# Reciprocals of softmax totals as powers on GpSimd instead of reciprocals on VectorE

## The chip, the core and the metric

The kernel runs on one NeuronCore of a Trainium2 chip. Its engines run their own instruction queues side by side and wait for each other through semaphores: TensorE (PE in the profile; its weight loads are PEld), VectorE (DVE), ScalarE (ACT), GpSimd (POOL), and SyncE (SP), which issues nearly all DMAs here. The metric is the device time of one execution in microseconds. Before the change it is 3157.24 us, the median of three runs (3157.11, 3157.24 and 3159.02).

## What is computed

Two attention blocks stand one after the other, on x of shape (8, 512, 32, 32) in float32: 8 batch items, 512 channels, 1024 positions. The change touches the softmax of the first block, which has 8 heads of 64 channels.

```python
# layer 0
hn = group_norm(x, gn1_scale, gn1_bias)              # 32 groups
qkv = einsum('bchw,oc->bohw', hn, w_qkv) + b_qkv
q, k, v = split(qkv.reshape(b * 8, 3 * 64, 1024), 3, axis=1)
wgt = softmax(einsum('bct,bcs->bts', q * 64 ** -0.25, k * 64 ** -0.25), axis=-1)
a = einsum('bts,bcs->bct', wgt, v)
x = x + group_norm(einsum('bchw,oc->bohw', a, w_proj) + b_proj, gn2_scale, gn2_bias)
# layer 1: weights normalised by row, qkv divided by its root mean square over
# channels, one head of 512 channels, softmax over 1024 positions
x = (x + w_out @ attention(x)) * 2 ** -0.5
```

## The kernel before

The kernel goes through the 8 batch items one after the other. For each it runs 32 steps of the first block's attention, then the first block's output projection and norm, then the second block; the steps of the next item begin while the last products of the second block are still being made. Every instruction is pinned to the order in which the program issues it on its engine (class InOrder, so most instructions carry its line, L34), and the order across engines comes from semaphores alone.

**A step.** Step i is one block of 128 query positions of one pair of heads: 4 pairs times 8 blocks make the 32 steps (STEPS, NB = 8). The two heads of a pair lie in the upper and lower 64 partitions of the queries and keys (tile qk) and are the two halves, hh = 0 and 1, of everything that follows. The method `step` (lines 635 to 650) issues, in this order:

- `softmax(i)`: for each head, VectorE takes the maximum of the scores in PSUM over 1024 keys, negated (TENSOR_REDUCE, nm<-s); ScalarE writes the exponentials to the tile p (128 partitions, both heads, 1024 keys each) and sums them into one column of the tile tot (called tt in the profile) by its accumulator. The accumulator comes out with a short instruction of its own behind the exponential, ACTIVATION_READ_ACCUMULATOR.
- `values(g)`, every second step: the products of values and transposed weights (po<-pT,v) for the two steps that were five and four steps back (LAG = 5).
- fills: a share of the projections that make the queries and keys of the next pair of heads, or leftovers of the second block.
- `scores(i + 1)`: TensorE's eight matmuls for the next step's scores, into two of three PSUM tiles (ps_s, three buffers).
- `turn()`: VectorE transposes the weights of the step before, in blocks of 32x32, from p into the tile pb (STREAM_TRANSPOSE, 128x2048), and SyncE copies them by four DMAs into pT.
- `scale()`: the weights of this step are multiplied by the reciprocals of their totals. VectorE makes the reciprocals of both heads, and GpSimd makes one scaling for each head (TENSOR_SCALAR, p<-p,tt).
- later work: additions on GpSimd that finish the queries and keys of the next pair (qk<-qk, qk<-qk,v, qk<-qk,spare), the normalisation of the next item's input (hn<-hn,a,c), and in the last eight steps of an item sums for the next item's values (tv<-hn, tv<-hn,tv).

So on VectorE the order in a step is: two maxima, the transposition of the step before, the reciprocal. On GpSimd it is: two scalings, then the later work, in one queue. The transposition of step i is issued in step i + 1, behind that step's maxima, and it waits for both scalings of step i.

**Buffers.** p and pb have two buffers each, the totals and negated maxima three each. The exponentials of step i + 2 go into the p of step i, which the transposition must have read.

**Pairs of heads.** Queries and keys of the next pair are put together on GpSimd in the last steps of the pair before, from pieces that ScalarE copies out of PSUM (`project_seven`, from the second batch item on; the first item and each item's first pair use `project_rows`, with fewer additions). TensorE's scores of the next pair's first step read them.

Of the kernel before, what the change touches and what calls it, by code (L numbers as in the profile page):

```python
# [8 lines left out]
F32 = mybir.dt.float32  # L9
I32 = mybir.dt.int32  # L10
AF = mybir.ActivationFunctionType
ALU = mybir.AluOpType
AX = mybir.AxisListType
P = 128
# [38 lines left out]
def attention_blocks_kernel(  # L53
# [38 lines left out]
    const = ctx.enter_context(tc.tile_pool(name="const", bufs=1))  # L92
# [12 lines left out]
    PE, VE, AC, PO, SY = (InOrder(tc, e) for e in (nc.tensor, nc.vector, nc.scalar, nc.gpsimd, nc.sync))  # L105
# [81 lines left out]
    for g in range(P // SQ):  # L187
        VE.tensor_copy(same[:, g * SQ : (g + 1) * SQ], flat)
    VE.tensor_scalar_mul(same2, same, 2.0 ** 0.5)
    shift = const.tile([P, 1], F32, name="shift")  # L190
    VE.memset(shift, -16.0)
    cols = const.tile([P, NCOLS], F32, name="cols")
# [79 lines left out]
    def turn(wrows, dst, k, scale=1.0):  # L272

        for half in range(2):
            pt = ps_s.tile([P, 2, CI, P], F32, tag="sc", name=f"wT_{k}_{half}")
            for jj in range(2):
                for ci in range(CI):
                    PE.transpose(pt[:, jj, ci, :], wrows[:, 2 * half + jj, ci * P : (ci + 1) * P], ident)
            o = dst[:, :, 2 * half * P : 2 * (half + 1) * P].rearrange("p ci (jj o) -> p jj ci o", jj=2)
            for jj in range(2):  # L280
                if jj:
                    AC.activation(o[:, jj], pt[:, jj], AF.Copy, scale=scale)
                else:
                    VE.tensor_scalar_mul(o[:, jj], pt[:, jj], scale)
# [267 lines left out]
    class Heads:  # L552
# [49 lines left out]

        def scale(self):
            i, p, tot = self.now
            VE.reciprocal(tot, tot)
            for hh in range(2):
                PO.tensor_scalar(p[:, :, hh, :], p[:, :, hh, :], tot[:, hh : hh + 1], 1.0, ALU.mult, ALU.mult)
            self.waiting = (i, p)

# [310 lines left out]
    class Layer1:  # L920
# [10 lines left out]
        def project(self, hn_next):  # L931
# [45 lines left out]
            def score_unit(m):  # L977

                w = near["score"]
                c = {f"{i + 1}{th + 1}": u[:, m + 2 * i, halves_[th]] for i in range(2) for th in range(2)}  # L980

                def last(which):
                    def scale(to=c[which], by=rrow[:, halves_[int(which[1]) - 1]]):
                        PO.tensor_mul(to, to, by)

                    if self.rrow is None:
                        waiting.append(scale)
                    else:
                        scale()

                return Seven(
                    f"u_{b}_{m}", HN,
                    lambda k, h: w[:, k, h, m * P : (m + 1) * P], self.right(slice(0, HN)), c, last,
                )
# [622 lines left out]
```

## Time and profile before

The profile is of one execution, which took 3158.3 us; its span from the first to the last instruction is 3156.5 us.

| engine | busy us | share of the span | instructions |
|---|---|---|---|
| TensorE, matmuls (PE) | 3128.6 | 99% | 13014 |
| TensorE, weight loads (PEld) | 1613.1 | 51% | 13014 |
| VectorE (DVE) | 2366.4 | 75% | 3213 |
| GpSimd (POOL) | 1409.5 | 45% | 1129 |
| ScalarE (ACT) | 1070.1 | 34% | 1844 |

The groups of instructions that the steps are made of, over all 256 steps:

| instruction | engine | count | busy us | mean ns |
|---|---|---|---|---|
| maximum, nm<-s, 128x1024 | VectorE | 512 | 602.2 | 1217 |
| transposition, pb<-p, 128x2048 | VectorE | 256 | 590.0 | 2305 |
| reciprocal, tt<-tt, 128x2 | VectorE | 256 | 32.2 | 126 |
| exponential, p<-s,nm, 128x1024 | ScalarE | 512 | 565.6 | 1109 |
| scaling, p<-p,tt, 128x1024 | GpSimd | 512 | 566.0 | 1118 |

How to read what follows: a line of the timeline begins with the start in microseconds from the span's start and the length; several like instructions in a row are merged, with their number behind an x. In brackets stands the idle time of the engine before the instruction and what ended it. A line of a stretch has its bounds, its length, the busy time of the engine with the number of instructions, the granted TensorE clock as a share of full speed, the busy share of the DMA engines and what they moved in GB/s. The granted clock is 0.998 over the span.

The second batch item's first maximum starts at 488.58 us and that of its last step at 657.45 us.

### The profile page before, as it was taken

How to read it: one execution, taken by the hardware profiler on the slowest of the kernel's cores; microseconds unless marked ns; L12 is line 12 of the kernel's file. 1: busy time of each engine (PE TensorE's matmuls, PEld its weight loads, DVE VectorE, ACT ScalarE, POOL GpSimd, SP SyncE). 2: the span in 40 equal slices, each digit the busy share in tenths (PEclk: the TensorE clock that was granted, in tenths of full speed). 3: DMA queues.
4: the chain of work that ended last, by engine and by line, in shares of the span. 5: the costliest groups of instructions: out<-in, count | busy, mean ns of one | idle time of the engine just before them, and what ended most of it. 6: DMA issues, size and time to landing. Idle time of an engine off the chain costs nothing.

```text
span 3156.5 us, 36568 instructions
## 1 busy us (share of the span) xinstructions
PE 3128.6 (99%) x13014; PEld 1613.1 (51%) x13014; DVE 2366.4 (75%) x3213; ACT 1070.1 (34%) x1844; POOL 1409.5 (45%) x1129
## 2 busy tenths in 40 slices
PE   9999999999999999999999999999999999999899
PEld 5445544456444554545545555445554455444454
DVE  5697777876788767886678876787677877778765
ACT  2453124521245212551125502354133531245311
POOL 1554236732367314771247703566235642356124
PEclk9999999999999999999999999999999999999999
DMA  6777225862168521784128832388224872158600
GB/s 207 208 203 232 77 57 158 215 203 67 57 180 230 178 55 60 206 231 153 47 79 227 225 117 51 114 219 227 91 68 119 217 230 77 30 159 213 194 7 33
DMA packets 230317, 451.56 MB, mean 143 GB/s; under 512 B 22100, under 2 KB 62840, under 8 KB 224376
## 3 DMA queue, kind: packets, MB, share of 16 engines
q1 hardware_dynamic: 230016, 449.20, 50.4%
q8 instruction: 104, 1.70, 0.2%
q14 instruction: 77, 0.63, 0.1%
q10 hardware_dynamic: 120, 0.02, 0.0%
HBM read 137.26 MB, written 29.56 MB: 53 GB/s over the span
## 4 chain that ended last, share of the span: by engine, by line
PE 88%; DMA 3%; POOL 3%; DVE 3%; SPq 1%; issue 1%; ACT 0%; DVEq 0%; ACTq 0%; POOLq 0%
PE s L34 12%; PE po L34 12%; PE p L34 7%; PE p_v_T L34 6%; PE pq L34 6%; PE p_v_B L34 5%; PE py L34 4%; PE pqk L34 4%; PE pa L34 4%; PE p_u_T L34 4%; PE pe_e L34 3%; PE pe_bc L34 3%; PE pe_a L34 3%; PE p_o_T L34 3%; PE p_u_B L34 3%; DMA pT<-pb 2%
## 5 line engine op out<-in xcount | busy, mean ns | idle before, releaser
L34 ACT ACTIVATE p<-s,nm 128x1024 f32<-128x1024 f32 x512 | 565.6, 1109 | 796.0 <-DVE nm L34 461.0
L34 POOL TENSOR_SCALAR p<-p,tt 128x1024 f32<-128x1024 f32 x512 | 566.0, 1118 | 413.5 <-DVE tt L34 405.4
L34 DVE TENSOR_REDUCE nm<-s 128x1 f32<-128x1024 f32 x512 | 602.2, 1217 | 138.1 <-PE s L34 137.0
L34 DVE STREAM_TRANSPOSE pb<-p 128x2048 f32<-128x2048 f32 x256 | 590.0, 2305 | 54.7 <-DMA pT<-pb 36.2
L34 PE MATMUL s<-qk 64*128 64x512 f32 x2048 | 510.5, 605 | 0.7 <-POOL qk L34 0.5
L34 PE MATMUL po<-pT,v 128*64 128x256 f32 x4096 | 473.4, 383 | 2.4 <-DMA pT<-pb 1.5
L34 PEld LDWEIGHTS po<-pT,v 128*64 128x64 f32 x4096 | 283.2, 137 | 228.5 <-issue 29.9
L34 PEld LDWEIGHTS s<-qk 64*128 64x128 f32 x2048 | 193.2, 186 | 242.7 <-issue 214.5
L34 PE MATMUL p<-e,v 128*128 128x512 f32 (+1 forms) x520 | 229.9, 594 | 2.5 <-DVE x L34 2.5
L34 POOL TENSOR_TENSOR x<-x,o 128x1024 f32<-128x1024 f32 x21 | 52.1, 2509 | 349.0 <-ACT o L34 349.0
L34 POOL TENSOR_TENSOR esum<-esum,e 128x512 f32<-128x512 f32 x96 | 141.6, 1499 | 148.3 <-ACT e L34 148.3
L34 POOL TENSOR_TENSOR u<-u,xy 128x512 f32<-128x512 f32 x64 | 79.2, 1268 | 278.1 <-DMA xy<-far_rinv 273.5
L34 PE MATMUL pq<-hn,qk 64*128 64x512 f32 (+1 forms) x420 | 191.8, 593 | 0.0
L34 ACT ACTIVATE e<-e,shift,rinv 128x512 f32<-128x512 f32 x96 | 75.8, 810 | 269.0 <-DVE e L34 269.0
L34 DVE TENSOR_TENSOR v<-v,p_v_T 128x256 f32<-128x256 f32 x300 | 114.3, 416 | 68.8 <-PE p_v_T L34 50.0
L34 PEld LDWEIGHTS p<-e,v 128*128 128x128 f32 x520 | 98.1, 192 | 130.5 <-issue 121.3
L34 PE MATMUL pqk<-hn,qk 64*128 64x512 f32 (+1 forms) x672 | 158.2, 590 | 0.0
L34 PE MATMUL pq<-t,qk 64*128 64x512 f32 x336 | 151.0, 589 | 0.0
L34 PE MATMUL pq<-v,qk 64*128 64x512 f32 x336 | 150.9, 589 | 0.0
L34 POOL TENSOR_TENSOR esum<-e 128x512 f32<-128x512 f32 x16 | 25.1, 1586 | 274.7 <-ACT e L34 274.7
L34 PE MATMUL py<-x,gram 128*128 128x512 f32 x320 | 141.2, 601 | 4.4 <-DVE x L34 4.4
L34 POOL TENSOR_TENSOR qk<-qk,v 128x512 f32<-128x512 f32 x96 | 127.2, 1334 | 3.2 <-ACT v L34 1.6
(240 smaller groups left out, 4737.7 us busy)
## 6 DMA issues: line engine op xcount, KB each, us to landing
pT<-pb SPq DMA_DIRECT2D x1024, 256.0 KB, 4.6
qk<-far_qk SPq DMA_DIRECT2D x21, 896.0 KB
hn<-in_x_dram SPq DMA_DIRECT2D x32, 512.0 KB, 4.8
x<-in_x_dram SPq DMA_DIRECT2D x32, 512.0 KB, 3.9
out_dram<-x SPq DMA_DIRECT2D x63, 256.0 KB, 2.8
score<-far_score SPq DMA_DIRECT2D x8, 1792.0 KB, 11.8
value<-far_value SPq DMA_DIRECT2D x8, 1792.0 KB
proj<-far_proj SPq DMA_DIRECT2D x7, 1792.0 KB
```

Source lines behind the costliest of these rows:

```text
L34: return lambda *args, **kw: self._pin(call(*args, **kw))
```

## The change

The reciprocal on VectorE is gone. In its place GpSimd raises each head's total to the power -1, one TENSOR_TENSOR on 128x1 against a constant column of -1.0, in front of that head's scaling. Each power waits for ScalarE's accumulator of its own head; each scaling waits for the power in front of it on the same engine. The constant is filled once by GpSimd at the start.

```diff
@@ constants
     VE.tensor_scalar_mul(same2, same, 2.0 ** 0.5)
+    minus = const.tile([P, 1], F32, name="minus")
+    PO.memset(minus, -1.0)
     shift = const.tile([P, 1], F32, name="shift")
     VE.memset(shift, -16.0)
@@ class Heads
         def scale(self):
             i, p, tot = self.now
-            VE.reciprocal(tot, tot)
             for hh in range(2):
+                PO.tensor_tensor(tot[:, hh : hh + 1], tot[:, hh : hh + 1], minus, ALU.pow)
                 PO.tensor_scalar(p[:, :, hh, :], p[:, :, hh, :], tot[:, hh : hh + 1], 1.0, ALU.mult, ALU.mult)
             self.waiting = (i, p)
```

The order of the other instructions on each engine stays as it was. Waits that the reciprocal's wait for ScalarE had covered move to other instructions: nearly all of VectorE's maxima now name ScalarE beside TensorE, for a negated maximum that ScalarE read three steps before.

## The prediction

> **What bounds the kernel now.** I read the page from the top: engine shares first, then the chain that ended last, then the group of instructions that the change touches.
>
> ```profile
> PE 3128.6 (99%) x13014; PEld 1613.1 (51%) x13014; DVE 2366.4 (75%) x3213; ACT 1070.1 (34%) x1844; POOL 1409.5 (45%) x1129
> ...
> PE 88%; DMA 3%; POOL 3%; DVE 3%; SPq 1%; issue 1%; ACT 0%; DVEq 0%; ACTq 0%; POOLq 0%
> ...
> L34 POOL TENSOR_SCALAR p<-p,tt 128x1024 f32<-128x1024 f32 x512 | 566.0, 1118 | 413.5 <-DVE tt L34 405.4
> ```
>
> PE is busy for 99% of the span and makes 88% of the chain. Nothing that another engine does faster can bring much: PE's idle time is 3156.5 - 3128.6 = 27.9 us in all. The third line is what the change aims at: POOL stands idle for 405 us in front of its scalings, and the reciprocals (tile tt) end that wait. The views of waits say whether anyone pays for it.
>
> ```profile
> POOL p L34 <- DVE tt L34: 405.4, 198, 9.5
> ...
> PEld s L34 <- ACT p L34: 13.6, 36, 0.9
> ...
> PEld s L34 <- POOL qk L34: 5.1, 11, 0.8
> ```
>
> Columns: us in total, times, longest. POOL's wait is long, but PE's weight loads for the scores wait for the softmax only 13.6 us in the whole kernel, and 5.1 us for the additions that POOL makes on queries and keys. So POOL's 405 us are slack, not loss, and the question turns round: how much of that slack do the added instructions use up? One steady step, from the timeline (start, length, engine):
>
> ```profile
> 649.05 2.30 DVE L34 STREAM_TRANSPOSE pb<-p 128x2048 f32<-128x2048 f32 x1
> 651.28 0.12 DVE L34 RECIPROCAL tt<-tt 128x2 f32<-128x2 f32 x1
> ...
> 654.58 2.30 DVE L34 STREAM_TRANSPOSE pb<-p 128x2048 f32<-128x2048 f32 x1
> ...
> 649.84 1.27 POOL L34 TENSOR_TENSOR tv<-hn,tv 128x512 f32<-128x512 f32 x1
> 651.50 2.21 POOL L34 TENSOR_SCALAR p<-p,tt 128x1024 f32<-128x1024 f32 x2 [0.39 <-DVE tt L34]
> ...
> 650.20 0.20 ACT L34 ACTIVATION_READ_ACCUMULATOR p<-s,nm 128x1 f32 x1
> ```
>
> The totals of both heads are out at 650.40; the reciprocal starts at 651.28 because the transposition stands ahead of it. Scaling ends at 653.71, and the transposition that reads its result starts at 654.58, 0.87 us later.
>
> **Removed.** 256 reciprocals of 0.12 us from DVE. Next on DVE are the maxima, which in steady steps wait for PE's scores anyway, so nothing is won there. In the few steps after a change of head pair, where DVE runs without pause, the reciprocal overlaps its neighbours and costs about 0.06 us (651.28 against the transposition's end at 651.35, then to 651.40); steps there last 4.7 us, 935.34 to 940.04 from maximum to maximum; some five of them in seven batch items give 35 x 0.06 = 2 us. The ceiling of any gain through the softmax is the 13.6 us above.
>
> **Moved.** The first scaling no longer waits for the transposition before it. No DMA is issued by the step itself; SP's copies follow the transposition as before, and PE's order is untouched. The scaling now runs beside the transposition: the addition at 649.84 lies wholly inside the one at 649.05 and takes 1.27 us, the common length of such additions, so I charge nothing for it. The Trainium skill (GPSIMD Engine Reference, section Key points) speaks against the move: GpSimd shares its SBUF interfaces with VectorE and contends with some of its instructions. Taken at its worst, scaling would be held until the transposition ends, nothing would start earlier, and the powers would come on top in full; the row above shows no such hold for an addition, and none shows it for a scaling.
>
> **Added.** One memset at the start (beside the weight loads, nothing), and 512 powers on 128x1, each followed by a scaling that must see its result. That hand-over costs 0.08 us: the additions x<-x,v read what the instruction before them wrote, and 30 of them have 2.4 us of idle time in front. The power itself is in no row. Lower end: an addition of no width.
>
> ```profile
> L34 POOL TENSOR_TENSOR x<-x,v 128x512 f32<-128x512 f32 x30 | 38.4, 1281 | 2.4
> ...
> L34 POOL TENSOR_TENSOR s_qk<-qk 64x2048 f32<-64x2048 f32 x1 | 4.5, 4526 | 0.0
> ```
>
> From about 1.27 us at 512 columns to 4.53 at 2048 the line rises 2.12 ns a column and meets zero at 0.18 us (its long row has half the partitions). A power is far more than an addition, so 0.18 is the floor. Upper end: 1.27 us, a whole 512-column addition; a power on one column would then cost as much as some 500 additions on a column. No row says where between them it lies; I take the middle, 0.73 us, so c = 0.81 us for a power with its hand-over (ends 0.26 and 1.35).
>
> The Trainium skill prices no power. Its table in GPSIMD Engine Reference, Elementwise — side-by-side cycle accounting, puts GpSimd at 1.96 times VectorE for an addition; twice the reciprocal's 0.12 us would be 0.24 us, c = 0.32, and the sum below would come to 3155 us.
>
> **POOL's idle time against c.** Stretches of the second batch item's 32 steps, cut at ends of scalings (length, POOL busy):
>
> ```profile
> 112.94:284.26 171.32, 101.76 (x91) 1.00 0.80 213
> 494.80:517.45 22.65, 16.60 (x14) 1.00 0.49 134
> 517.45:538.28 20.83, 16.84 (x15) 1.00 0.84 215
> 538.28:580.18 41.90, 29.30 (x26) 1.00 0.83 223
> 580.18:621.70 41.52, 29.30 (x26) 1.00 0.84 216
> 621.70:664.38 42.68, 32.52 (x29) 1.00 0.87 240
> ```
>
> The first line is the first batch item, 31 steps; the others have 3, 4, 8, 8 and 8 steps with two powers each. Idle: 6.05, 3.99, 12.60, 12.22, 10.16 us. At c = 0.81 the powers need 4.86, 6.48, 12.96, 12.96, 12.96: short by 0, 2.49, 0.36, 0.74, 2.80. A stretch that is short is late by as much: the transposition waits for the scaling, the maxima queue behind it on DVE, the exponentials behind those, and the next scores find no free PSUM; the cover is the 0.87 us above, once.
>
> A second clock runs at each change of head pair, where POOL makes the new queries and keys:
>
> ```profile
> 612.34 1.55 POOL L34 TENSOR_TENSOR qk<-qk,v 128x512 f32<-128x512 f32 x1
> 614.34 2.21 POOL L34 TENSOR_SCALAR p<-p,tt 128x1024 f32<-128x1024 f32 x2 [0.45 <-DVE tt L34]
> 616.51 2.51 POOL L34 TENSOR_TENSOR qk<-qk,v 128x512 f32<-128x512 f32 x2
> ...
> 618.27 1.99 PE L34 MATMUL s<-qk 64*128 64x512 f32 x8
> ```
>
> The first addition at 616.51 ends at 617.8 and PE reads it at 618.27. Started as early as its data allow (601.5, when the exponentials of the third step before are out), POOL then has three scalings (6.63), four additions (2.89 and 2.82) and the first of the last two (1.25): it ends at 615.1 + 6c. It must end by 618.2, so c may be 0.52; at 0.81 PE waits 1.7 us, at three changes in each of seven items.
>
> Taking the larger of the two in the second to fourth full stretch: 2.49 + 1.74 + 1.74 + 2.80 = 8.8 us an item. Six items like this give 53; the last, without the sums of the final stretch, 6; the first, with 69.6 us idle for 62 powers, only its last stretch, 2. Sum +61, less 2 for the reciprocals. The profiled execution took 3158.3 us (span 3156.5), 1 us over the median of 3157.24; on the median: **3216 us**.
>
> **Rivals.** (A) The power fits: c at most 0.5. Then no stretch is short, the changes of pair hold, and only the 2 us are left: 3155 us, at the most 3144 if all 13.6 us went. For it: the floor of 0.18, and 45 us of idle for 62 powers in an item, 0.73 each. Against it: a power is no addition. It decides at c = 0.52. (C) The power costs more than a 512-column addition: at c = 2.0 an item is short by 62 x 2.0 - 45 = 79, six times, and 54 and 58 in the first and last (idle 69.6 and 65.5): 3157 + 586 = 3743 us. For it: no row shows POOL doing more than additions, products, copies and fills. Against: one column is very little data. My forecast is (B), between: at c = 1.35 an item is short by 38.7, the first and last by 14 and 18: +264, 3419 us.
>
> **How the numbers follow.** A 0.34, B 0.47, C 0.19. A measurement of this kernel tells about 0.2% from no change, 6 us (its three runs lie within 2 us). A gives faster 0.07 and same 0.27, since 2 us cannot be seen and 6 would need half the ceiling; B and C are slower, 0.66. The forecast's own range is 3160 to 3419. The range for 8 in 10 takes in A and all of B: 3148 to 3430; C and the best of A are left out.
>
> **What would show it.** A TENSOR_TENSOR tt<-tt,minus group on POOL gives d at once: near 0.2 to 0.4 A holds, near 0.7 B, over 1.3 C. With B, POOL's waits for tt vanish, waits of DVE's transposition for POOL p and of PE for POOL qk grow, and steps 24 to 31 lengthen from 5.33 us (42.68 over 8). The forecast is wrong if the power is cheap, if a scaling beside a transposition is longer than 1.12 us, or if PE covers late scores with other work.

## The result and the profile after

| kernel | median us | lowest to highest | runs | ratio to before |
|---|---|---|---|---|
| before | 3157.54 | 3157.11 to 3159.02 | 4 | 1 |
| changed | 3181.19 | 3179.65 to 3182.98 | 4 | 1.0075 (1.0063 to 1.0088) |

The change costs 23.65 us, 0.75%. The profiled execution took 3180.18 us, with a span of 3178.4, 21.9 us more than before; the granted clock is 0.998 in both.

The page of the changed kernel: engine shares, chain of waits, and the groups that the change touches (busy us, mean ns of one, idle us in front and what ended most of it).

```profile
span 3178.4 us, 37566 instructions
...
PE 3129.9 (98%) x13014; PEld 1627.0 (51%) x13014; DVE 2354.3 (74%) x2957; ACT 1065.6 (34%) x1844; POOL 1681.9 (53%) x1642
...
PE 60%; POOL 24%; issue 9%; DMA 3%; DVE 2%; ACT 1%; SPq 0%; POOLq 0%; DVEq 0%; ACTq 0%
...
L34 DVE STREAM_TRANSPOSE pb<-p 128x2048 f32<-128x2048 f32 x256 | 590.3, 2306 | 92.1 <-POOL p L34 73.2
L34 POOL TENSOR_SCALAR p<-p,tt 128x1024 f32<-128x1024 f32 x512 | 572.3, 1118 | 50.5
L34 PE MATMUL s<-qk 64*128 64x512 f32 x2048 | 510.7, 605 | 21.4 <-POOL qk L34 21.4
...
L34 POOL TENSOR_TENSOR tt<-tt,minus 128x1 f32<-128x1 f32 x512 | 281.2, 549 | 115.2 <-ACT p L34 115.2
```

PE has the same work (3129.9 us against 3128.6), so its idle time went from 27.9 to 48.5 us: nearly the whole loss is PE standing still. POOL, at 3% of the chain before, is now 24% of it. The last line prices the new operation: a power lasts 0.549 us. Scaling is as long as before, 1118 ns.

The waits of the changed kernel (us in total, times, longest):

```profile
POOL tt L34 <- ACT p L34: 115.2, 81, 7.4
...
DVE pb L34 <- POOL p L34: 73.2, 77, 3.4
...
PEld s L34 <- POOL qk L34: 30.9, 21, 2.3
...
PE s L34 <- POOL qk L34: 21.4, 21, 1.8
...
DVE pb L34 <- DMA pT<-pb: 16.4, 17, 1.9
```

Three of these waits before the change:

```profile
DVE pb L34 <- DMA pT<-pb: 36.2, 31, 4.0
...
DVE pb L34 <- POOL p L34: 15.0, 10, 2.3
...
PE s L34 <- POOL qk L34: 0.5, 2, 0.4
```

POOL's wait of 405.4 us for the reciprocal is gone; it now waits 115.2 us for ScalarE's totals. Two waits grew in its place: PE waits 21.4 us for queries and keys, 21 times, where it waited 0.5; the transposition waits 73.2 us for the scalings, where it waited 15.0. The first looks like the whole loss and the second like far more than it. The experiments show that the second is no price, and that removing the first need not bring it back. Of the 21.4 us, 12.7 lie at the first change of pair of the seven items, 3.8 at the second and 4.9 at the third.

Where the time went, from the starts of each step's first maximum (us, sums over batch items 2 to 8; the first item and what has no steps in columns of their own). Rows of the experiments are put beside it for later:

| kernel | steps 0, 1 | 2 to 7 | 8 to 15 | 16 to 23 | 24 to 30 | first item | between items | head and tail |
|---|---|---|---|---|---|---|---|---|
| before | 113.7 | 225.2 | 298.9 | 291.3 | 261.1 | 174.4 | 1479.6 | 312.3 |
| changed | 113.7 | 241.9 | 297.2 | 296.0 | 261.7 | 174.1 | 1480.3 | 313.4 |
| e1, one power a step | 113.7 | 232.7 | 297.2 | 294.2 | 261.7 | 180.2 | 1478.3 | 312.2 |
| e2, first half of a pair | 113.7 | 232.6 | 294.6 | 290.8 | 261.7 | 174.1 | 1478.3 | 310.2 |
| e3, second half of a pair | 113.7 | 229.7 | 300.7 | 295.9 | 261.7 | 174.0 | 1478.2 | 313.2 |
| e4, products for powers | 113.7 | 224.8 | 294.1 | 290.8 | 261.6 | 177.3 | 1478.0 | 312.9 |
| e5, powers twice | 113.7 | 294.3 | 336.0 | 333.9 | 295.4 | 182.5 | 1507.3 | 309.9 |
| e6, an addition on VectorE | 113.7 | 237.8 | 301.5 | 295.1 | 260.3 | 174.1 | 1480.7 | 312.8 |
| e7, e1 without the first item | 113.7 | 232.4 | 297.6 | 293.8 | 261.7 | 173.9 | 1478.4 | 310.1 |
| e8, few powers | 113.7 | 224.5 | 294.1 | 291.0 | 261.4 | 173.9 | 1478.7 | 311.6 |
| e9, first pair only | 113.7 | 242.0 | 294.3 | 291.2 | 261.1 | 173.9 | 1478.5 | 312.2 |
| e10, other pairs only | 113.7 | 224.6 | 298.2 | 296.1 | 261.7 | 173.9 | 1479.4 | 312.1 |
| e11, four steps only | 113.7 | 224.3 | 296.1 | 290.8 | 261.5 | 173.9 | 1478.6 | 312.1 |

In this table the loss sits in two places: 16.7 us in steps 2 to 7, the rest of the first pair of heads (2.4 an item), and 4.7 us in steps 16 to 23. Steps 8 to 15 vary between kernels that issue the same there (298.9 before, 294.3 in e9), so differences of up to 5 us in that column are read with care. That variation is in steps 9 and 10 above all: 83.7 us over the seven items before and 77.8 in e9. It goes with the transposition's wait for the copies out of pb, in step 10 17.2 us before and 12.6 in e9. The column hides the second change of pair: step 15 takes 5.52 us before and 6.13 in the changed kernel, in the mean of seven items, which is another 4.3 us lost.

The first pair of the second batch item on the changed kernel's timeline: POOL, and the matmuls and transpositions that wait for it.

```profile
502.10 0.55 POOL L34 TENSOR_TENSOR tt<-tt,minus 128x1 f32<-128x1 f32 x1 [3.14 <-ACT p L34]
...
505.56 1.27 POOL L34 TENSOR_TENSOR v<-v,esum 128x512 f32<-128x512 f32 x1
...
534.56 0.55 POOL L34 TENSOR_TENSOR tt<-tt,minus 128x1 f32<-128x1 f32 x1
535.20 1.12 POOL L34 TENSOR_SCALAR p<-p,tt 128x1024 f32<-128x1024 f32 x1
536.28 2.49 POOL L34 TENSOR_TENSOR qk<-qk,v 128x512 f32<-128x512 f32 x2
...
537.60 1.99 PE L34 MATMUL s<-qk 64*128 64x512 f32 x8 [1.81 <-POOL qk L34]
...
530.04 2.31 DVE L34 STREAM_TRANSPOSE pb<-p 128x2048 f32<-128x2048 f32 x1 [0.76 <-POOL p L34]
...
536.35 2.31 DVE L34 STREAM_TRANSPOSE pb<-p 128x2048 f32<-128x2048 f32 x1 [1.76 <-POOL p L34]
```

POOL's last pause is at 502.10: it waits 3.14 us for a total, while the work left over from the second block (v<-v,esum and x<-x,v) stands behind that power in its queue. From 505.56 on it runs through until the pair has changed, as the view of this stretch says (bounds, length, POOL's busy time with its instructions, clock, DMA share, GB/s):

```profile
505.56:541.10 35.54, 33.97 (x36) 1.00 0.68 184
```

33.97 of 35.54 us are busy, and the remaining 1.57 are pauses of a tenth of a microsecond between dependent instructions. The addition that PE needs begins at 536.28, right behind a scaling; PE reads it at 537.60 after 1.81 us without work. The transposition at 536.35 is late by 1.76 us for the same reason.

A steady step of the changed kernel, to be held against the one shown of before:

```profile
653.06 2.30 DVE L34 STREAM_TRANSPOSE pb<-p 128x2048 f32<-128x2048 f32 x1
655.24 0.56 POOL L34 TENSOR_TENSOR tt<-tt,minus 128x1 f32<-128x1 f32 x1
655.89 1.12 POOL L34 TENSOR_SCALAR p<-p,tt 128x1024 f32<-128x1024 f32 x1
656.98 0.56 POOL L34 TENSOR_TENSOR tt<-tt,minus 128x1 f32<-128x1 f32 x1
657.63 1.12 POOL L34 TENSOR_SCALAR p<-p,tt 128x1024 f32<-128x1024 f32 x1
...
658.78 2.31 DVE L34 STREAM_TRANSPOSE pb<-p 128x2048 f32<-128x2048 f32 x1
```

The scalings end at 658.75 and the transposition begins at 658.78, with no wait named: here the powers just fit. From the power's start to the scaling's are 0.65 us (0.549, and 0.099 of hand-over in the median of 512); a pair of power and scaling takes 1.73 us where a scaling alone takes 1.09 before the change, so one power costs POOL 0.64 us.

### The profile page after: what moved, and what is told of

It reads as the page before. It is cut to its first block, busy times and chain, and to the rows that moved or that the text cites. A ratio compares the mean times of both kernels' runs of the same rounds, so it can differ in the third digit from the quotient of the medians.

```text
span 3178.4 us, 37566 instructions
## 1 busy us (share of the span) xinstructions
PE 3129.9 (98%) x13014; PEld 1627.0 (51%) x13014; DVE 2354.3 (74%) x2957; ACT 1065.6 (34%) x1844; POOL 1681.9 (53%) x1642
## 4 chain that ended last, share of the span: by engine, by line
PE 60%; POOL 24%; issue 9%; DMA 3%; DVE 2%; ACT 1%; SPq 0%; POOLq 0%; DVEq 0%; ACTq 0%
POOL p L34 11%; PE p_v_T L34 6%; PE po L34 5%; POOL tt L34 5%; PE s L34 5%; PE py L34 4%; PE p_v_B L34 4%; PE pqk L34 4%; POOL qk L34 4%; PE p_u_T L34 3%; PE pe_e L34 3%; PE pe_bc L34 3%; PE pe_a L34 3%; PE p_o_T L34 3%; PE pa L34 3%
## 5 line engine op out<-in xcount | busy, mean ns | idle before, releaser
L34 DVE TENSOR_REDUCE nm<-s 128x1 f32<-128x1024 f32 x512 | 601.4, 1216 | 151.8 <-PE s L34 151.4
L34 DVE STREAM_TRANSPOSE pb<-p 128x2048 f32<-128x2048 f32 x256 | 590.3, 2306 | 92.1 <-POOL p L34 73.2
L34 POOL TENSOR_SCALAR p<-p,tt 128x1024 f32<-128x1024 f32 x512 | 572.3, 1118 | 50.5
L34 PE MATMUL s<-qk 64*128 64x512 f32 x2048 | 510.7, 605 | 21.4 <-POOL qk L34 21.4
L34 POOL TENSOR_TENSOR tt<-tt,minus 128x1 f32<-128x1 f32 x512 | 281.2, 549 | 115.2 <-ACT p L34 115.2
```

The source lines that it names most:

```text
L34: return lambda *args, **kw: self._pin(call(*args, **kw))
```

## The experiments

The edits are shown against the changed kernel. Before was timed again beside each group: 3157.48 us for e1 to e4, 3157.97 for e5 to e8, 3157.70 for e9 to e11 (20 to 22 runs each). Two readings of the loss stood against each other at first. In one, P in the expectations, powers cost where PE waits for queries and keys at a change of pair. In the other, T, they cost in every stretch where the transposition waits for the scalings, so that total waiting of the transposition prices them.

**e1, one power a step.** Both heads in one instruction.

```diff
-    minus = const.tile([P, 1], F32, name="minus")
+    minus = const.tile([P, 2], F32, name="minus")
...
+            PO.tensor_tensor(tot, tot, minus, ALU.pow)
             for hh in range(2):
-                PO.tensor_tensor(tot[:, hh : hh + 1], tot[:, hh : hh + 1], minus, ALU.pow)
```

> One power on 128x2 for both heads instead of two on 128x1; it must wait for the second head's exponential, 1.1 us later than the first power did. Theory P (the loss of 23.7 us is TensorE's wait for GpSimd's additions on queries and keys at the 21 changes of head pair, late because two powers a step are queued ahead of them): GpSimd has 0.65 us less to do in a step, TensorE's wait for POOL qk falls from 21.4 us to under 5, time 3155 to 3163 us. Theory T (the loss arises in every step, where the transposition waits for the later end of scaling, 73.2 us against 15.0): the scalings end 0.45 us later than with two powers where GpSimd is free and earlier where it is not, so the loss stays above 15 us, time 3172 us or more.

3171.23 us, 1.0043 (1.0028 to 1.0058). A power on two columns lasts 0.70 us, so a step has 0.40 us less of powers than the changed kernel's 1.10, and one hand-over fewer. The steps of items 2 to 8 are 11.0 us shorter than in the changed kernel, and PE's wait for queries and keys fell to 9.7 us, not under the 5 that P gave. The first batch item, whose steps the change had left at their length, is 5.8 us longer than before (180.2 against 174.4); e7 and the last section come back to it. The time lies between the two forecasts, and without these 5.8 us it would still be 2 us above P's.

**e2 and e3, half of the steps each.** Powers in the first four steps of each pair, VectorE's reciprocal in the others; and the reverse.

```diff
+            power = i % NB < NB // 2          # e3: i % NB >= NB // 2
+            if not power:
+                VE.reciprocal(tot, tot)
             for hh in range(2):
-                PO.tensor_tensor(tot[:, hh : hh + 1], tot[:, hh : hh + 1], minus, ALU.pow)
+                if power:
+                    PO.tensor_tensor(tot[:, hh : hh + 1], tot[:, hh : hh + 1], minus, ALU.pow)
```

> Powers in the first four steps of each pair of heads, VectorE's reciprocal in the last four, where GpSimd makes the next pair's queries and keys. Theory P: GpSimd's queue in front of the change of pair is as it was before the change but for its start; TensorE's wait for POOL qk falls to 5 us or less (before: 0.5), time 3154 to 3161 us. Theory T (a loss in each step that has powers): half of the loss stays, 3169 us.

> The complement: reciprocals in the first four steps of each pair, powers in the last four. Theory P: nearly the whole loss stays, TensorE's wait for POOL qk over 12 us, time 3170 to 3182 us. Theory T: half of the loss, 3169 us, with TensorE's wait for POOL qk no more than half of 21.4 us.

e2: 3159.75 us, 1.0007 (0.9997 to 1.0017). e3: 3167.46 us, 1.0029 (1.0017 to 1.0041). The same two waits in e2:

```profile
DVE pb L34 <- POOL p L34: 46.8, 37, 2.3
...
PE s L34 <- POOL qk L34: 3.5, 7, 0.6
```

and in e3:

```profile
DVE pb L34 <- POOL p L34: 33.2, 50, 2.5
...
PE s L34 <- POOL qk L34: 14.5, 21, 1.0
```

With as many powers in each, e2 loses 2 us, as P had it, and e3 10; that is 2.5 us under P's range and 1.5 under T's forecast, with PE's wait over the 12 us of P. The transposition waits longer in e2, PE in e3: the loss goes with PE's wait, and the transposition's total is no price. But the two parts add up to 12 us, not to 24. What is lost depends on how many powers stand in the same busy stretch; in e2's seven first pairs the first four steps alone, with leftovers of the second block, already cost 7.4 us in steps 2 to 7, and PE waits at that change only.

**e4, products in place of powers.** The same instruction with a cheap operation. The weights are multiplied by minus their totals, so this kernel leaves the reciprocals out.

```diff
-                PO.tensor_tensor(tot[:, hh : hh + 1], tot[:, hh : hh + 1], minus, ALU.pow)
+                PO.tensor_tensor(tot[:, hh : hh + 1], tot[:, hh : hh + 1], minus, ALU.mult)
```

> The power becomes a product on the same 128x1 operands: the weights are scaled by minus their total instead of its reciprocal, so the reciprocals are left out of the computation; instructions, waits and order are those of the changed kernel. It measures what of the 0.549 us is the power and what any instruction of this shape costs: 0.18 to 0.30 us expected for the product. Theory P: with a hand-over of 0.1 us each instruction costs 0.3 to 0.4 us, below the 0.52 us at which the changes of pair become late, TensorE's wait for POOL qk under 2 us, time 3153 to 3159 us; anything clearly below 3157.5 is what the earlier scaling is worth when its reciprocal costs little. Theory T: half of the added work, so about half of the loss, 3167 to 3170 us.

3154.07 us, 0.9992 (0.9982 to 1.0001). The product lasts 0.190 us, so 0.36 of the power's 0.549 are the power itself. Then PE does not wait for queries and keys, steps 2 to 7 take 224.8 us as before (225.2), and the kernel is level with before or a few microseconds faster. So in items 2 to 8 the move from VectorE to POOL, the extra waits and the instructions cost nothing, and the length of the power costs it all. The first item is 2.9 us longer than before; the last section shows why that may be.

**e5, each power twice.** A power with a result that nothing reads, in front of each.

```diff
+    scratch = const.tile([P, 1], F32, name="scratch")
...
             for hh in range(2):
+                PO.tensor_tensor(scratch, minus, minus, ALU.pow)
                 PO.tensor_tensor(tot[:, hh : hh + 1], tot[:, hh : hh + 1], minus, ALU.pow)
```

> A second power on constants, written to a scratch column, in front of each power: 0.55 us more of GpSimd for each of 512, nothing else. Each head then costs GpSimd about 1.18 us in place of 0.63. By the sum of the prediction (an item is short by 62 x 1.18 less its idle time of 45 us; 69.6 and 65.5 us in the first and last) the kernel is GpSimd-bound in the steps: 6 x 28 + 4 + 8 = 180 us, time 3337 us; 3310 to 3360 us if that way of pricing is right. If the loss were a matter of TensorE's wait at the changes of pair alone (theory P without the idle time running out), 21 changes x 6 x 0.55 us more = 69 us on top of 3181, time 3250 us.

3371.17 us, 1.0676 (1.0661 to 1.0690). The extra power takes 0.52 us from its start to the next one's. Its waits:

```profile
DVE pb L34 <- POOL p L34: 263.8, 138, 4.7
...
PE s L34 <- POOL qk L34: 91.3, 21, 5.0
```

The first 512 powers cost 24 us, the next 512 cost 190, of which 27 lie between the items. Now every stretch of steps is longer, the last one by 34 us as well, which the changed kernel had left alone. That is what idle time runs out like: cheap up to the limit of each stretch, at full price past it. A price at the changes of pair alone would have ended far below, near 3250 us. In the steps of the second to seventh item POOL is busy for 187.8 of some 196.5 us. The time is 34 us above the expectation, and most of that is growth between the items (28 us over before), where only the last step of each has powers. The granted clock was 0.979 over the span, 0.95 to 0.97 in the steps of items 2 to 8 and 0.98 to 1.00 between the items; why it was lower was not followed up, nor how much of the 190 us comes from it.

**e6, one addition at the change of pair on VectorE.** It takes from POOL the addition that PE waits for.

```diff
-                ([add(q1, q1, tmp[0]), add(q2, q2, tmp[1])], [add(q2, q2, tmp[2])]),
+                ([lambda: VE.tensor_add(q1, q1, tmp[0]), add(q2, q2, tmp[1])], [add(q2, q2, tmp[2])]),
```

> The changed kernel, with one addition at each change of pair (the one that completes the first half of the queries) on VectorE instead of GpSimd; powers and scalings as in the change. Theory P: what TensorE waits for at the change is then the keys, which GpSimd finishes one scaling pair earlier, and VectorE's addition of 0.68 us; the wait for POOL qk (21.4 us) goes to under 6 us, time 3156 to 3166 us. Theory T (transpositions late by GpSimd in every step): unchanged, 3176 us or more. If VectorE's addition is held by a scaling that runs beside it, as its 128x4 instructions were in the run with one power for both heads (1.0 us in place of 0.16), it lasts 1.0 to 1.8 us and a part of the loss stays.

3175.73 us, 1.0054 (1.0040 to 1.0068): the wait was removed, and 18 of the 24 us stayed. Waits of e6:

```profile
DVE pb L34 <- POOL p L34: 68.3, 58, 3.5
...
DVE pb L34 <- DMA pT<-pb: 46.4, 42, 2.9
...
PEld s L34 <- ACT p L34: 21.6, 57, 0.9
```

PE no longer waits for queries and keys anywhere. In its place PE's weight loads wait 21.6 us for the softmax (10.6 in the changed kernel), and the transposition waits still. At the first change of pair, where PE had waited 12.7 us, steps 2 to 7 won back only 4.1 of their 16.7 us. There PE's wait for the additions had been the first to pay for a late POOL, not the cause: with it relieved, the next in line pays. So P as first stated is wrong for the first pair, and a third reading, B in what follows, took its place: POOL's queue is full in the stretch, and whoever waits for POOL first pays. At the other two changes the loss did go with PE's wait: step 15 takes 5.52 us (5.52 before, 6.13 in the changed kernel) and step 23 takes 5.78 (5.62 and 6.29). What e6 loses behind them goes with another wait, that of the transposition for the copies out of pb: 46.4 us, against 16.4 in the changed kernel.

The edit also has a price of its own. The addition lasts 0.85 us in the mean, 17.9 us over 21 changes, about as much as stayed. Yet behind 20 of the 21 additions the transposition still waits 0.49 to 1.13 us for POOL, so that the addition's own length is covered there. But it stretches 14 powers by 6.6 us in all, 3.2 of them at the first change, and so makes POOL later. How much of the 18 us is the edit's own price was not separated further. Where it met a power, the power was long (e6's timeline):

```profile
531.44 1.13 DVE L34 TENSOR_TENSOR qk<-qk,v 128x512 f32<-128x512 f32 x1
531.98 1.00 POOL L34 TENSOR_TENSOR tt<-tt,minus 128x1 f32<-128x1 f32 x1
```

**e7, e1 from the second item on.** One power for both heads, with the two columns of e1's constant, and in the first item the reciprocal.

```diff
+            if self.b:
+                PO.tensor_tensor(tot, tot, minus, ALU.pow)
+            else:
+                VE.reciprocal(tot, tot)
             for hh in range(2):
-                PO.tensor_tensor(tot[:, hh : hh + 1], tot[:, hh : hh + 1], minus, ALU.pow)
```

> One power on 128x2 for both heads from the second batch item on, VectorE's reciprocal in the first. In the run with one power everywhere (3171.2 us) the first item's steps took 180.2 us against 174.4 before, where eleven of VectorE's 128x4 instructions lasted 1.0 us beside a scaling. If these held instructions are the first item's loss, it goes back to 174 to 175 us with none of them over 0.2 us, time 3165 to 3167 us. If the first item's loss is the power's own time on GpSimd, the two are not tied to each other: steps come back only in part while other items stay as they were.

3165.42 us, 1.0025 (1.0015 to 1.0035), where it was expected. The first item is back at 173.9 us and 5.8 us of e1's loss are gone with it. Of the rest, 7.2 us sit in the first pair.

**e8, powers where POOL has room.** In the first four steps of the second to fourth pair, from the second item on: 84 of 256 steps.

```diff
+            power = self.b > 0 and NB <= i and i % NB < NB // 2
+            if not power:
+                VE.reciprocal(tot, tot)
             for hh in range(2):
-                PO.tensor_tensor(tot[:, hh : hh + 1], tot[:, hh : hh + 1], minus, ALU.pow)
+                if power:
+                    PO.tensor_tensor(tot[:, hh : hh + 1], tot[:, hh : hh + 1], minus, ALU.pow)
```

> Powers only in steps 8 to 11, 16 to 19 and 24 to 27 of the second to last batch items, reciprocals in all others: the stretches after a change of pair, where VectorE runs without pause and GpSimd has most idle time; the first pair, which lost 1.3 us an item in the run with powers in the first half of every pair, keeps its reciprocals. Theory P: no wait of TensorE for POOL qk beyond the 0.5 us of before, VectorE 12 reciprocals shorter an item in its tight steps, time 3154 to 3158 us, at best 0.1% below the kernel before. Theory T: 84 of 256 steps have powers, so a third of the loss, 3165 us.

3150.79 us, 0.9978 (0.9969 to 0.9987) over 11 runs: faster than both kernels, 7 us under before. Chain and scores on its page:

```profile
PE 96%; DVE 1%; POOL 1%; DMA 1%; SPq 0%; issue 0%; ACT 0%; DVEq 0%; ACTq 0%; POOLq 0%
...
L34 PE MATMUL s<-qk 64*128 64x512 f32 x2048 | 503.4, 605 | 0.1
```

PE's matmuls no longer wait for POOL, and PE makes 96% of the chain. The transposition's waits for scalings, 16.4 us, all lie in the last step of an item, as nearly all of before's 15.0 do. The gain is larger than was expected. It sits in steps 8 to 15 (294.1 against 298.9), but e9 reaches 294.3 there with no powers in them, so that it comes from these powers at this place isn't shown. What e8 and e9 share are shorter steps 9 and 10 (78.3 and 77.8 us, before 83.7) and, in step 10, a shorter wait of the transposition for the copies out of pb (10.9 and 12.6 us, before 17.2); why the wait is shorter is open.

**e9 and e10, the first pair against the others.** Powers from the second item on, only in the first pair; or only in the other three.

```diff
+            power = self.b > 0 and i < NB          # e10: i >= NB
+            if not power:
+                VE.reciprocal(tot, tot)
             for hh in range(2):
-                PO.tensor_tensor(tot[:, hh : hh + 1], tot[:, hh : hh + 1], minus, ALU.pow)
+                if power:
+                    PO.tensor_tensor(tot[:, hh : hh + 1], tot[:, hh : hh + 1], minus, ALU.pow)
```

> Powers only in the first eight steps (the first pair of heads) of the second to last batch items, reciprocals elsewhere: 56 of 256 steps. Theory B, formed from the runs so far: the loss comes where GpSimd's queue has no idle time left, which is the first pair, whose steps also carry the second block's leftover products; whatever waits for GpSimd first pays, TensorE for queries and keys or VectorE's transposition. Steps 2 to 7 of the seven items keep nearly all of the 16.7 us that they lost with the full change (225.2 to 241.9 us): time 3171 to 3177 us. Rival E, each of the three changes of pair loses alike: a third of 23.7 us, 3165 us. Rival T, each power costs alike: 56/256 of it, 3163 us.

> The complement in the same items: powers in steps 8 to 31, reciprocals in the first pair. Theory B: the steps keep what they had with the full change, -1.7 us in steps 8 to 15, +4.7 in 16 to 23, +0.6 after: 3158 to 3163 us. Rival E: two thirds of 23.7 us, 3173 us. Rival T: 168/256, 3173 us.

e9: 3168.59 us, 1.0034 (1.0021 to 1.0047). e10: 3162.92 us, 1.0018 (1.0009 to 1.0027). A quarter of the steps brings 10.9 us, the other three quarters 5.2. e9's time is 2.4 us under the range that B gave, because its steps 8 to 15 came out at 294.3; e10's lies in B's range. E and T gave 3173 us for e10 and fall by that. By stretches B holds in steps 2 to 7, which take 242.0 us in e9 and 224.6 in e10, the changed kernel's 241.9 and before's 225.2, and in steps 16 to 23, with 291.2 and 296.1, again before's and the changed kernel's. It did not foresee e9's steps 8 to 15.

**e11, four steps an item.** Powers in steps 8 to 11 only, the part of e8 that lies at the second pair.

```diff
+            power = self.b > 0 and NB <= i < NB + NB // 2
+            if not power:
+                VE.reciprocal(tot, tot)
             for hh in range(2):
-                PO.tensor_tensor(tot[:, hh : hh + 1], tot[:, hh : hh + 1], minus, ALU.pow)
+                if power:
+                    PO.tensor_tensor(tot[:, hh : hh + 1], tot[:, hh : hh + 1], minus, ALU.pow)
```

> Powers only in steps 8 to 11 of the second to last batch items, 28 of 256 steps: where the run with few powers (3150.8 us) had its gain, 298.9 to 294.1 us over steps 8 to 15, if that is the whole of it. Then steps 8 to 15 come to 294 to 295 us here too and the time to 3151 to 3155 us. If the gain is spread over all steps with powers, a third of 7.2 us stays: 3155.6 us, steps 8 to 15 over 296 us.

3152.15 us, 0.9980 (0.9971 to 0.9989). With a third of e8's powers it has the most of e8's gain. The time lies in the range of the first expectation, but steps 8 to 15 take 296.1 us, which is what the second gave, so the place of the gain stays open; that a few powers in these steps go with a kernel 0.2% faster is what both runs show.

## Why the prediction was right in its mechanism and too high in size

**The bound.** Right: PE's work is unchanged, and the loss is idle time of PE that POOL's lateness makes. POOL's 405 us in front of the scalings were slack, as the prediction said: in e4 nothing waits for VectorE's reciprocals any more, and its median is 3 us under before.

**Removed and moved.** "Charge nothing" for a scaling beside the transposition held: of the changed kernel's scalings, 94 lie wholly inside a transposition and last 1117 ns in the median, as long as the others, and the transposition is 2306 ns against 2305. The reciprocals were priced at 2 us. e4 removes them at the least new cost and stands 0 to 6 us below before by its interval, so the term is of the right size or a few microseconds small.

**The power: the failing step.** "I take the middle, 0.73 us, so c = 0.81 us for a power with its hand-over". Measured are 0.549 and 0.099, and a cost to POOL of 0.64, where 0.81 was put. The middle between 0.18 and 1.27 was a choice without a row, and the sum is steep there: with 0.64 in the prediction's own stretches, steps 2 to 7 are short by 1.13 us, the second and third change late by 6 x (0.64 - 0.52) = 0.72 each, and the last stretch, with 16 x 0.64 = 10.24 us against 10.16 idle, by 0.08. That is 2.65 us an item, 19 in seven, and with the 2 us off 3174 where 3216 was forecast and 3181 measured.

**The stretches.** With the measured c the form of the two clocks is nearly right. The last stretch had been put at 2.80 us an item and shows under 0.1, just as 10.24 against 10.16 says. Steps 16 to 23 lost 0.67 us an item against the 0.72 of the change of pair. Step 15, the other such change, lost 0.61, though steps 8 to 15 as a whole are 1.7 us shorter than before because of steps 9 and 10. Only the first pair was taken too lightly, 2.4 us an item against 1.13, which is 9 us of the time. The prediction counted all of POOL's idle time in its first stretches, 6.05 + 3.99 = 10.04 us, as room. But 3.14 us of it is the wait for a total at 502.10, with the leftovers queued behind; what stands in a queue can't use the time in front of the instruction it waits behind. That leaves 6.9 us for 14 powers, 0.49 each, and 14 x 0.64 - 6.9 = 2.1 us late. That the 3.14 us are the reason is read from the trace and its sum; no run moved the leftovers ahead. That the first pair is where the loss sits was shown by e9 and e10.

**The rivals.** A needed c under 0.52; at 0.64 it falls, by little, and e4, whose instruction is 0.19 us, shows that it was right about the kernel such an instruction would give. C needed a power over 1.27 us and falls by the row of 0.549. e5 shows the mechanism that C priced: at c = 0.64 + 0.52 = 1.16 the prediction's form 62 x 1.16 - 45 gives 162 us for six items and 9 for the first and last, and the steps grew by 191, at the lower clock named there.

**The signs named beforehand.** POOL's waits for VectorE's reciprocals vanished, and the transposition's waits for scalings and PE's for queries and keys grew. Steps 24 to 31 did not lengthen, which is the smaller c again.

## What to carry to other kernels

An engine at 45% can be full where it matters: count the idle time of each stretch between two events that another engine waits for, and leave out idle time in front of an instruction that itself waits, with the work queued behind it. A wait that grows by just the loss is the first payer and need not be the cause: at the first change of pair e6 took 12.7 us of waiting away and won back 4.1. When the one price that decides is in no row, say at which value the sum turns steep, here c = 0.52; here a power for each head went to GpSimd without a loss only in the steps that have room for it.

## What the hardware showed beside this

In e1 the first batch item grew by 5.8 us with no wait to explain it. Small VectorE instructions met a scaling there (timeline of e1, VectorE, then POOL):

```profile
214.15 1.00 DVE L34 TENSOR_TENSOR rs<-rs,ve 128x4 f32<-128x4 f32 x1
215.18 1.06 DVE L34 SCALAR_TENSOR_TENSOR a<-rs,a 128x4 f32<-128x4 f32 x1
...
214.02 2.22 POOL L34 TENSOR_SCALAR p<-p,tt 128x1024 f32<-128x1024 f32 x2
```

The same two took 0.16 us each before, where the scaling could not start until the reciprocal behind them was done. In e1 each lasts until the scaling beside it ends. Six of the 144 instructions on these tiles are held in e1 and five in e4 (first item 177.3 us), or eleven and eight with all others of shape 128x4, but none in the changed kernel, whose powers happen to stand beside them:

```profile
213.18 0.16 DVE L34 TENSOR_TENSOR rs<-rs,ve 128x4 f32<-128x4 f32 x1
213.38 0.16 DVE L34 SCALAR_TENSOR_TENSOR a<-rs,a 128x4 f32<-128x4 f32 x1
...
212.86 0.55 POOL L34 TENSOR_TENSOR tt<-tt,minus 128x1 f32<-128x1 f32 x1
```

Nine of the 144 begin beside a power in the changed kernel and none lasts over 0.165 us. In the other direction, e6's power beside VectorE's addition took 1.00 us in place of 0.55. Transpositions and the maxima from PSUM were not held by scalings: in the changed kernel they last 2306 and 1216 ns beside one, as they do elsewhere. That the held instructions are what lengthens the first item is argued, not isolated: it fits that e7, with reciprocals there and no instruction held, takes 173.9 us, and that the changed kernel, with more power time and none held, takes 174.1. So taking an operation off VectorE can remove an order that had kept its neighbours clear of GpSimd.

The Trainium skill (SBUF — State Buffer, section SBUF: two separate sides) says that VectorE and GpSimd share a pair of ports as an exclusive lock: a VectorE instruction with two SBUF inputs and a GpSimd instruction that reads SBUF block each other for the whole instruction. The scalings and e6's addition agree, with 1.00 us for 0.16 and for 0.55; the powers of the changed kernel do not, since instructions of 0.16 us begin and end within one of 0.55.
